# Layer 0's attention: the softmax row sums of two stretches formed in one visit of TensorE

## The chip, the cores and the metric

The kernel runs on one core of one Trainium2 chip, in float32 throughout. The metric is the device time of one execution in microseconds (us). Five engines matter: TensorE (PE, with its weight loads as PEld), VectorE (DVE), ScalarE (ACT), GpSimd (POOL) and the DMA queue that SyncE feeds (SP).

## The reference

Two attention blocks are applied one after the other to 8 images of 512 channels and 1024 positions. The change lies in the first, "layer 0", which has 8 heads of 64 channels:

```python
h = group_norm(x, gn_weight, gn_bias)
qkv = jnp.einsum('oc,bct->bot', w_qkv, h.reshape(B, C, T)) + b_qkv[None, :, None]
...
weight = jnp.einsum('bct,bcs->bts', q * scale, k * scale)
weight = jax.nn.softmax(weight.astype(jnp.float32), axis=-1).astype(weight.dtype)
a = jnp.einsum('bts,bcs->bct', weight, v)
...
out = jnp.einsum('oc,bct->bot', w_proj, a) + b_proj[None, :, None]
return x + out.reshape(B, C, H, W)
```

Layer 1 is of the same kind with one head of 512 channels. The change touches its code only in the form of one call.

## The kernel before

Each image goes through layer 0's attention, the projection, layer 1's products for the image before, and the keys, queries and values for the next one. The four channel tiles of an image hold two heads each. `attention0` (L604) works through 8 stretches per image: a pair of heads hp (0 to 3) by a half of the 1024 positions tb (0 or 1). For hp 0, 1 and 2 the order is tb 0, tb 1; for hp 3 it is tb 1, tb 0. I write a stretch as (hp, tb).

A stretch has two parts on TensorE. First, for each of 8 blocks of 128 keys, it forms the scores `sc` of both heads, each matmul using 64 rows and 128 columns of the array; ScalarE turns them into `e` by Exp (L621), and VectorE adds up the eight `e` tiles into `total` (L623 for the first two, L625 for the rest). Then `av` (128 rows by 64 columns of the array) multiplies `e` by the values and accumulates over the 8 blocks; ScalarE copies it into the channel tile `a` (L639), still without its division by the row sums.

The division goes through `reciprocals` (L575). Four matmuls with `ones` (128 rows by 32 columns) sum `total` over its partitions into one PSUM tile, `sums`, and leave each 128 positions on another group of 32 partitions. VectorE takes the reciprocal (L586), and keeps the smallest (L587, `low_recs`); POOL adds all up (L588, `all_recs`). Both serve a test at the kernel's end. The reciprocals go to DRAM (`rows`, L590) and come back as a broadcast over partitions, `r`, by two DMAs (L600). POOL multiplies `a` by `r` (L644); for the very last stretch of an image, (3, 0), VectorE does so later, and the DMAs go through ScalarE's queue.

Each fp32 matmul stands in the profile as two records: a stretch has 32 records of `sc`, 32 of `av` and 8 of `sums`. Matmuls on different parts of the array run side by side: `sc` and `av` in pairs, `sums` in fours.

The order on TensorE is that of the program, since `matmul` (L67) pins it. Behind the scores and behind `av` of each stretch there is a place for further steps, `extra`: among them, differences of the next operands on VectorE (L1068, `t_h`, `h` and `t_a`), two at a time. On each engine and on the SP queue the instructions stand in program order; a wait on one holds up all behind it.

Tiles come from pools. `total`, `e`, `a` and the operands share one pool of 32 buffers (`big`); `av` and `sums` share two PSUM buffers (`acc`); `rc` and `r` have two buffers each, and `rows` has three.

Of the kernel before, what the change touches and what calls it, by code (L numbers as in the profile page):

```python
# [9 lines left out]
F32 = mybir.dt.float32  # L10
I32 = mybir.dt.int32
AF = mybir.ActivationFunctionType
ALU = mybir.AluOpType
AX = mybir.AxisListType

P = 128
# [13 lines left out]
def two_attention_blocks_kernel(  # L30
# [8 lines left out]
    nc = tc.nc  # L39
    B, C, T = x.shape  # L40
    KC = C // P
    HT = T // 2
# [12 lines left out]
    ones = const.tile([P, P], F32, name="ones")  # L55
# [4 lines left out]
    low_recs = const.tile([P, 2, P], F32, name="low_recs")  # L60
    nc.vector.memset(low_recs, 1.0)
    all_recs = const.tile([P, 2, P], F32, name="all_recs")
# [3 lines left out]
    def matmul(*args, **kw):  # L66
        tc.keep_in_program_order(nc.tensor.matmul(*args, **kw))  # L67
# [108 lines left out]
    def main_path(ctx):  # L176
# [3 lines left out]
        rpool = ctx.enter_context(tc.tile_pool(name="rpool", bufs=2))  # L180
        rowpool = ctx.enter_context(tc.tile_pool(name="rows", bufs=3, space=bass.MemoryType.DRAM))
# [3 lines left out]
        def big_tile(name, shape=(P, T)):  # L185
            return big.tile(list(shape), F32, tag="big", name=name)

        def pair_tile(name):
            return big_tile(name, (P, 2, HT))

        def acc_tile(name):
            return ps_acc.tile([P, HT], F32, tag="acc", name=name)
# [143 lines left out]
        def weight(n):  # L336
            return weight_factors(weight_part(n))
# [53 lines left out]
        def channel_tiles(name):  # L391
            return [big_tile(f"{name}_{c}") for c in range(KC)]
# [23 lines left out]
        def query_factors(f, uid):  # L416

            t = big_tile(f"inner_{uid}", (P, 4, 2 * P))
            s1, s2, s3, s4 = (t[:, i, :] for i in range(4))
            a11, a21, a12, a22 = (f[k][:, ts(i, 2 * P)] for k in range(2) for i in range(2))  # L420
            for dst, x, y, op in (
                (s1, a21, a22, ALU.add), (s2, s1, a11, ALU.subtract), (s3, a11, a21, ALU.subtract),
                (s4, a12, s2, ALU.subtract),
            ):

                tc.keep_in_program_order(nc.gpsimd.tensor_tensor(dst, x, y, op))  # L426
            return {1: a11, 2: a12, 3: s4, 4: a22, 5: s1, 6: s2, 7: s3}
# [144 lines left out]
            return out  # L572


        def reciprocals(total, uid, across, queue=nc.sync):  # L575

            sums = acc_tile(f"sums_{uid}")[:, : 2 * P].rearrange("p (a b) -> p a b", a=2)
            for i in range(4):
                matmul(sums[ts(i, 32), :, :], ones[:, :32], total[:, :, ts(i, P)], start=True, stop=True)
            rc = rpool.tile([P, 2, P], F32, tag="rc", name=f"rc_{uid}")
            nc.vector.reciprocal(rc, sums)  # L586
            nc.vector.tensor_tensor(low_recs, low_recs, rc, ALU.min)  # L587
            nc.gpsimd.tensor_tensor(all_recs, all_recs, rc, ALU.add)  # L588
            rows = rowpool.tile([2, 4, P], F32, tag="rows", name=f"rows_{uid}")
            queue.dma_start(rows.rearrange("j i n -> i j n"), rc[0:P:32, :, :])  # L590
            if across:
                r = pair_tile(f"r_{uid}")
                for j in range(2):
                    row = rows[j : j + 1].rearrange("j i n -> j (i n)")
                    queue.dma_start(r[:, j, :], row.to_broadcast([P, HT]))
            else:
                r = rpool.tile([P, HT], F32, tag="r", name=f"r_{uid}")
                for j in range(2):
                    row = rows[j : j + 1].rearrange("j i n -> j (i n)")
                    queue.dma_start(r[ts(j, 64), :], row.to_broadcast([64, HT]))  # L600
            return r


        def attention0(b, q, k, v, a, extra):  # L604
            n = 0

            for hp in range(KC):
                for tb in (0, 1) if hp < KC - 1 else (1, 0):
                    uid = f"0_{b}_{hp}_{tb}"
                    total = pair_tile(f"sum_{uid}")  # L610
                    es = []
                    for s in range(NS):
                        sc = ps_pools[n % 3].tile([P, 2, HT], F32, tag="sc", name=f"sc_{uid}_{s}")
                        n += 1
                        for j in range(2):
                            matmul(
                                sc[:, j, :], k[hp][ts(j, 64), ts(s, P)], q[hp][ts(j, 64), ts(tb, HT)],
                                start=True, stop=True,
                            )
                        e = pair_tile(f"e_{uid}_{s}")  # L620
                        nc.scalar.activation(e, sc, AF.Exp, scale=(C // 8) ** -0.5)  # L621
                        if s == 1:
                            nc.vector.tensor_add(total, es[0], e)  # L623
                        elif s > 1:
                            nc.vector.tensor_add(total, total, e)  # L625
                        es.append(e)
                    for f in extra.pop(0) if extra else ():
                        f()
                    av = acc_tile(f"av_{uid}")
                    for s in range(NS):  # L630
                        for j in range(2):
                            matmul(
                                av[ts(j, 64), :], v[s // 2][:, s % 2, hp * P + j * 64 : hp * P + (j + 1) * 64],
                                es[s][:, j, :], start=(s == 0), stop=(s == NS - 1),
                            )
                    for f in extra.pop(0) if extra else ():
                        f()
                    dst = a[hp][:, ts(tb, HT)]
                    nc.scalar.copy(dst, av)  # L639

                    last = (hp, tb) == (KC - 1, 0)
                    r = reciprocals(total, uid, False, nc.scalar if last else nc.sync)
                    if not last:
                        nc.gpsimd.tensor_tensor(dst, dst, r, ALU.mult)  # L644
                    else:
                        scaled = lambda dst=dst, r=r: tc.keep_in_program_order(nc.vector.tensor_mul(dst, dst, r))

            assert not extra
            return scaled
# [277 lines left out]
        def load_again(b, c, what):  # L927
            t = big_tile(f"{what}_{b}_{c}")
            nc.sync.dma_start(t, spills[b][c])
            return t  # L930

        def all_background():
            run_background(len(background))
# [93 lines left out]
        def layer1_rest(b, hf, inner, gf, gsteps, stats, hooks, ahead):  # L1027
            if inner:
                first = query_factors(gf[1], f"1_1_{b}")
                total, ef = scores1_twice(b, inner, gf, gsteps, first, f"1_{b}", stats)  # L1030
            else:
                total, ef = scores1(b, gf, hf, f"1_{b}")
            state = {}

            def sums():
                state["r"] = reciprocals(total, f"1_{b}", True)

            z = by_token(
                weight("z"), hf, f"z1_{b}", hooks=[*hooks, [sums]], back=3,
                after=[load_weight, lambda: background.extend(zsteps)],  # L1040
            )
            all_background()
            xt = [load_again(b, c, "x") for c in range(KC)]
            stiles = [big_tile(f"sz{i}_{b}", (P, 2, 2, C // 2)) for i in (1, 2, 4)]
            halves = lambda t: (t[:, :, : C // 2], t[:, :, C // 2 :])
            zf, zsteps = left_sums(
                [halves(t) for t in z[:2]], [halves(t) for t in z[2:]],
                [lambda j, t=t: t[:, j, :, :] for t in stiles], nc.vector.tensor_add, nc.vector.tensor_sub,
            )
            values1(b, zf, ef, state["r"], xt, f"1_{b}", ahead)  # L1050

        for b in range(B):
# [13 lines left out]
            a = channel_tiles(f"a0_{b}")  # L1066
# [4 lines left out]
            if b > 0:  # L1071
                hf, t = image_factors(h, f"h1_{b - 1}", here)
                for i, fs in enumerate((t[:1], t[1:2], (t[2], t[4]), (t[6], t[3]), (t[5], t[7]), steps[:2], steps[2:4])):
                    extra[2 * i + 3] += fs
            elif B > 1:
                hf, t = image_factors(h, "h0_1", here)
# [3 lines left out]
            scaled = attention0(b, q, k, v, a, extra)  # L1080
# [5 lines left out]
            if b > 0:  # L1086
# [6 lines left out]
                _, _, mean, affine = norm_hooks(norm1, f"1_{b}")  # L1093
# [6 lines left out]
                if b + 1 < B:  # L1100
                    hf, steps = image_factors(h, f"h0_{b + 1}")
                    background.extend(steps)
                    v, f, norm0 = values(b + 1, hf)
                    q, k = keys_and_queries(b + 1, f, norm0, ())
            elif B > 1:
                v, f, norm0 = values(1, hf, [[], [], [], [], [*steps[:7], scaled, steps[7]]])
# [169 lines left out]
    with ExitStack() as main_ctx:  # L1276
        main_path(main_ctx)
# [45 lines left out]
```

## Time and profile before

| | |
|---|---|
| median of 3 runs | 2852.84 us (2851.77 to 2853.81) |
| profiled execution, its own time | 2852.44 us |
| its span, first to last instruction | 2850.6 us |
| granted TensorE clock, mean | 0.999 |
| Exp, L621 | 512 times, 1053 ns each |
| adds into `total`, L625 | 384 times, 1357 ns each |
| reciprocal, L586 | 72 times, 1756 ns each |
| `all_recs`, L588 | 72 times, 882 ns each |
| multiply by `r` on POOL, L644 | 56 times, 1943 ns each |

In the timelines that follow, a row is a run of like instructions: its start in us from the span's beginning, the time from its start to the end of its last instruction, engine, line, operation, what it writes and reads, and how many there were; in brackets, how long the engine was idle before it and what ended that. Matmuls are pipelined, so the row of one group reaches into the next; the starts tell more than the ends.

### The profile page before, as it was taken

What the parts mean: (1) busy time and instruction counts of PE and PEld (TensorE: products, weight loads), DVE (VectorE), ACT (ScalarE), POOL (GpSimd) and SP (SyncE); (2) the same over time, 40 slices, a digit from 0 to 9 for tenths busy, and PEclk for the clock granted to TensorE, in tenths of its full rate; (3) what the DMA queues carried; (4) which work ended last, traced back from release to release, by engine and by line L of the source; (5) the groups of instructions that cost most, each with busy time, mean ns of one, the idle gap of its engine ahead of it and who ended that gap; (6) DMA issues with size and microseconds to landing.
All of it is one profiled execution on the core that took longest, in us unless ns stands there. A gap on an engine that the chain in (4) does not pass through costs nothing.

```text
span 2850.6 us, 32020 instructions
## 1 busy us (share of the span) xinstructions
PE 2834.5 (99%) x11720; PEld 1665.7 (58%) x11720; DVE 2062.8 (72%) x2718; ACT 919.9 (32%) x1166; POOL 1106.2 (39%) x1110
## 2 busy tenths in 40 slices
PE   9999999999999999999999999999999999999999
PEld 5435635866367653677537674376833858348544
DVE  5587787766877678776787757877588775887654
ACT  1252452214522145221552215421163312533110
POOL 2113225732167322673127711377114761147100
PEclk9999999999999999999999999999999999999999
DMA  8722403133032231322213231122411224022201
GB/s 276 246 97 90 179 20 134 37 144 126 20 144 76 100 123 42 118 94 97 112 46 111 93 138 72 49 107 101 154 52 45 107 108 153 16 74 79 96 0 68
DMA packets 91594, 281.02 MB, mean 99 GB/s; under 512 B 10595, under 2 KB 36387, under 8 KB 82470
## 3 DMA queue, kind: packets, MB, share of 16 engines
q1 hardware_dynamic: 89638, 276.61, 26.5%
q10 hardware_dynamic: 1792, 2.29, 0.2%
q8 instruction: 95, 1.56, 0.2%
q14 instruction: 69, 0.57, 0.1%
HBM read 225.93 MB, written 52.93 MB: 98 GB/s over the span
## 4 chain that ended last, share of the span: by engine, by line
PE 98%; issue 1%; DVE 1%; POOL 0%; ACT 0%; DVEq 0%; POOLq 0%
PE sc L67 16%; PE av L67 16%; PE psb_av L67 6%; PE psb L67 5%; PE psa_av L67 4%; PE psc_av L67 4%; PE psc L67 3%; PE psa L67 3%; PE psb_z L67 3%; PE psb_p L67 3%; PE psb_v L67 3%; PE psb_g L67 3%; PE psb_k L67 3%; PE psb_q L67 2%; PE psa_p L67 2%; PE psa_z L67 2%
## 5 line engine op out<-in xcount | busy, mean ns | idle before, releaser
L625 DVE TENSOR_TENSOR sum<-sum,e 128x1024 f32<-128x1024 f32 x384 | 521.0, 1357 | 40.7 <-DVE sum L623 0.5
L621 ACT ACTIVATE e<-sc 128x1024 f32<-128x1024 f32 x512 | 476.8, 1053 | 73.4 <-PE sc L67 72.6
L67 PE MATMUL sc<-q,k 64*128 64x512 f32 x2048 | 458.7, 596 | 0.5
L67 PE MATMUL av<-e,v 128*64 128x512 f32 x2048 | 453.6, 595 | 0.0
L67 PEld LDWEIGHTS sc<-q,k 64*128 64x128 f32 x2048 | 193.2, 186 | 239.2 <-ACT e L621 104.0
L67 PEld LDWEIGHTS av<-e,v 128*64 128x64 f32 x2048 | 141.4, 137 | 304.3 <-issue 304.3
L588 POOL TENSOR_TENSOR all_recs<-all_recs,rc 128x256 f32<-128x256 f32 x72 | 63.5, 882 | 579.6 <-DVE rc L586 572.0
L644 POOL TENSOR_TENSOR a<-a,r 128x512 f32<-128x512 f32 x56 | 108.8, 1943 | 260.8 <-DMA r<-rows 246.5
L586 DVE RECIPROCAL rc<-sums 128x256 f32<-128x256 f32 x72 | 126.4, 1756 | 47.8 <-PE sums L67 26.6
L532 POOL TENSOR_TENSOR k<-k,k 128x256 f32<-128x256 f32 x28 | 20.0, 726 | 314.5 <-DVE u_k L527 314.5
L639 ACT COPY a<-av 128x512 f32<-128x512 f32 x64 | 37.4, 585 | 322.7 <-PE av L67 322.7
L623 DVE TENSOR_TENSOR sum<-e,e 128x1024 f32<-128x1024 f32 x64 | 78.4, 1226 | 59.3 <-ACT e L621 59.3
L67 PE MATMUL psa_av<-e,z 128*128 128x512 f32 x256 | 113.3, 595 | 0.0
L140 ACT ACTIVATE h<-h,b,s 128x1024 f32<-128x1024 f32 x62 | 78.5, 1270 | 87.2 <-DMA h<-in_x 70.6
L67 PE MATMUL psb<-inner,inner_h 128*128 128x256 f32 x392 | 101.6, 382 | 0.8
L411 POOL TENSOR_TENSOR inner_h<-h,inner_h 128x256 f32<-128x256 f32 x112 | 101.1, 905 | 2.2
L67 PEld LDWEIGHTS psb<-inner,inner_h 128*128 128x128 f32 x392 | 73.3, 190 | 14.9 <-POOL inner L426 3.4
L67 PEld LDWEIGHTS psa_av<-e,z 128*128 128x128 f32 x256 | 48.0, 190 | 57.3 <-issue 56.6
L411 POOL TENSOR_TENSOR inner_h<-h 128x256 f32<-128x256 f32 x56 | 55.4, 990 | 66.8 <-ACT h L140 66.8
L411 POOL TENSOR_TENSOR inner_h<-t_h 128x256 f32<-128x256 f32 x84 | 73.6, 879 | 10.8 <-PE psc_av L67 9.5
L67 PE MATMUL psb_g<-inner_h,w_m 128*128 128x256 f32 x294 | 75.1, 383 | 0.3
L67 PE MATMUL psb_q<-inner_h,w_q 128*128 128x256 f32 x294 | 75.4, 385 | 0.0
(382 smaller groups left out, 5435.2 us busy)
## 6 DMA issues: line engine op xcount, KB each, us to landing
x<-in_x SPq DMA_DIRECT2D x36, 512.0 KB
h<-in_x SPq DMA_DIRECT2D x32, 512.0 KB
spill<-x SPq DMA_DIRECT2D x32, 512.0 KB
h<-spill SPq DMA_DIRECT2D x32, 512.0 KB
x<-spill SPq DMA_DIRECT2D x32, 512.0 KB
out<-x SPq DMA_DIRECT2D x64, 256.0 KB
w_p<-sums_p SPq DMA_DIRECT2D x8, 1792.0 KB
r<-rows SPq DMA_DIRECT2D x112, 128.0 KB
```

The lines of the kernel that those rows point to most:

```text
L67: tc.keep_in_program_order(nc.tensor.matmul(*args, **kw))
L140: tc.keep_in_program_order(nc.scalar.activation(dst, src, AF.Identity, bias=b, scale=s))
L411: pin(nc.gpsimd.tensor_tensor(dst, x, y, ALU.subtract))
L532: nc.gpsimd.tensor_tensor(d, x, y, ALU.add)
L586: nc.vector.reciprocal(rc, sums)
L588: nc.gpsimd.tensor_tensor(all_recs, all_recs, rc, ALU.add)
L621: nc.scalar.activation(e, sc, AF.Exp, scale=(C // 8) ** -0.5)
L623: nc.vector.tensor_add(total, es[0], e)
L625: nc.vector.tensor_add(total, total, e)
L639: nc.scalar.copy(dst, av)
L644: nc.gpsimd.tensor_tensor(dst, dst, r, ALU.mult)
```

## The change

`reciprocals` takes a list of totals. For `n` of them it forms `n` groups of sums, side by side in one PSUM tile, and returns `n` tiles `r`. `attention0` keeps (`total`, `dst`) of the stretches (0, 0), (1, 0) and (2, 0), which are listed in `PAIRS_BEGUN`, and calls `reciprocals` for two totals after (0, 1), (1, 1) and (2, 1). Both stretches of hp 3 call it with one total, as before. Layer 1 calls it with one total.

```diff
-        def reciprocals(total, uid, across, queue=nc.sync):
+        def reciprocals(totals, uid, across, queue=nc.sync):
...
-            sums = acc_tile(f"sums_{uid}")[:, : 2 * P].rearrange("p (a b) -> p a b", a=2)
-            for i in range(4):
-                matmul(sums[ts(i, 32), :, :], ones[:, :32], total[:, :, ts(i, P)], start=True, stop=True)
-            rc = rpool.tile([P, 2, P], F32, tag="rc", name=f"rc_{uid}")
-            nc.vector.reciprocal(rc, sums)
-            nc.vector.tensor_tensor(low_recs, low_recs, rc, ALU.min)
-            nc.gpsimd.tensor_tensor(all_recs, all_recs, rc, ALU.add)
-            rows = rowpool.tile([2, 4, P], F32, tag="rows", name=f"rows_{uid}")
-            queue.dma_start(rows.rearrange("j i n -> i j n"), rc[0:P:32, :, :])
...
+            n = len(totals)
+            sums = acc_tile(f"sums_{uid}")[:, : n * 2 * P].rearrange("p (t a b) -> p t a b", t=n, a=2)
+            for t, total in enumerate(totals):
+                for i in range(4):
+                    matmul(sums[ts(i, 32), t, :, :], ones[:, :32], total[:, :, ts(i, P)], start=True, stop=True)
+            rs = []
+            for t in range(n):
+                rc = rpool.tile([P, 2, P], F32, tag="rc", name=f"rc_{uid}_{t}")
+                nc.vector.reciprocal(rc, sums[:, t, :, :])
+                nc.vector.tensor_tensor(low_recs, low_recs, rc, ALU.min)
+                nc.gpsimd.tensor_tensor(all_recs, all_recs, rc, ALU.add)
+                rows = rowpool.tile([2, 4, P], F32, tag="rows", name=f"rows_{uid}_{t}")
+                queue.dma_start(rows.rearrange("j i n -> i j n"), rc[0:P:32, :, :])
...
+                else:
+                    r = rpool.tile([P, HT], F32, tag="r", name=f"r_{uid}_{t}")
+                    for j in range(2):
+                        row = rows[j : j + 1].rearrange("j i n -> j (i n)")
+                        queue.dma_start(r[ts(j, 64), :], row.to_broadcast([64, HT]))
+                rs.append(r)
+            return rs
...
+        PAIRS_BEGUN = [(hp, 0) for hp in range(KC - 1)]
...
-                    last = (hp, tb) == (KC - 1, 0)
-                    r = reciprocals(total, uid, False, nc.scalar if last else nc.sync)
-                    if not last:
-                        nc.gpsimd.tensor_tensor(dst, dst, r, ALU.mult)
-                    else:
-                        scaled = lambda dst=dst, r=r: tc.keep_in_program_order(nc.vector.tensor_mul(dst, dst, r))
+                    unscaled.append((total, dst))
+
+                    if (hp, tb) not in PAIRS_BEGUN:
+
+                        last = (hp, tb) == (KC - 1, 0)
+                        rs = reciprocals([t for t, _ in unscaled], uid, False, nc.scalar if last else nc.sync)
+                        for (_, dst), r in zip(unscaled, rs):
+                            if not last:
+                                nc.gpsimd.tensor_tensor(dst, dst, r, ALU.mult)
+                            else:
+                                scaled = lambda dst=dst, r=r: tc.keep_in_program_order(nc.vector.tensor_mul(dst, dst, r))
+                        unscaled = []
...
-                state["r"] = reciprocals(total, f"1_{b}", True)
+                (state["r"],) = reciprocals([total], f"1_{b}", True)
```

The order of the instructions in the changed program follows from this and from a scheduler that fills engines in between. On VectorE, the two reciprocals of a pair stand first, then the two `low_recs`; on POOL, two `all_recs`, then two multiplies; on the SP queue, two `rows`, then the four `r`.

More of the change, by code (lines that the diff above doesn't have):

```diff
@@ L572, in conv2 @@
             return out
-        def reciprocals(total, uid, across, queue=nc.sync):
-            sums = acc_tile(f"sums_{uid}")[:, : 2 * P].rearrange("p (a b) -> p a b", a=2)
-            for i in range(4):
-                matmul(sums[ts(i, 32), :, :], ones[:, :32], total[:, :, ts(i, P)], start=True, stop=True)
-            rc = rpool.tile([P, 2, P], F32, tag="rc", name=f"rc_{uid}")
-            nc.vector.reciprocal(rc, sums)
-            nc.vector.tensor_tensor(low_recs, low_recs, rc, ALU.min)
-            nc.gpsimd.tensor_tensor(all_recs, all_recs, rc, ALU.add)
-            rows = rowpool.tile([2, 4, P], F32, tag="rows", name=f"rows_{uid}")
[L590 to L595, printed above, removed]
-            else:
[L597 to L601, printed above, removed]
@@ new lines, in reciprocals @@
+        def reciprocals(totals, uid, across, queue=nc.sync):
[12 more added lines that the diff above has]
+                queue.dma_start(rows.rearrange("j i n -> i j n"), rc[0:P:32, :, :])
+                if across:
+                    r = pair_tile(f"r_{uid}_{t}")
+                    for j in range(2):
+                        row = rows[j : j + 1].rearrange("j i n -> j (i n)")
+                        queue.dma_start(r[:, j, :], row.to_broadcast([P, HT]))
+                else:
+                    r = rpool.tile([P, HT], F32, tag="r", name=f"r_{uid}_{t}")
+                    for j in range(2):
+                        row = rows[j : j + 1].rearrange("j i n -> j (i n)")
+                        queue.dma_start(r[ts(j, 64), :], row.to_broadcast([64, HT]))
+                rs.append(r)
+            return rs
@@ L639, in attention0 @@
                     nc.scalar.copy(dst, av)
-                    last = (hp, tb) == (KC - 1, 0)
-                    r = reciprocals(total, uid, False, nc.scalar if last else nc.sync)
-                    if not last:
-                        nc.gpsimd.tensor_tensor(dst, dst, r, ALU.mult)
-                    else:
-                        scaled = lambda dst=dst, r=r: tc.keep_in_program_order(nc.vector.tensor_mul(dst, dst, r))
+                    unscaled.append((total, dst))
[7 more added lines that the diff above has]
+                                scaled = lambda dst=dst, r=r: tc.keep_in_program_order(nc.vector.tensor_mul(dst, dst, r))
+                        unscaled = []
             assert not extra
```

## The prediction, made before the changed kernel ran

> **What bounds the kernel now.** I read the busy times first, then the chain that ended last, then the timeline of one stretch, engine by engine.
>
> ```profile
> PE 2834.5 (99%) x11720; PEld 1665.7 (58%) x11720; DVE 2062.8 (72%) x2718; ACT 919.9 (32%) x1166; POOL 1106.2 (39%) x1110
> ...
> PE 98%; issue 1%; DVE 1%; POOL 0%; ACT 0%; DVEq 0%; POOLq 0%
> ```
>
> TensorE is the bound: every microsecond it gains or waits moves the end. The timeline of PE over stretch (3,1) of image 3, i.e. hp 3, tb 1, the one that follows the third pair:
>
> ```profile
> 1113.68 0.60 PE L67 MATMUL av<-e,v 128*64 128x512 f32 x2
> 1114.21 0.64 PE L67 MATMUL sums<-sum,ones 128*32 128x256 f32 x8
> 1114.78 7.14 PE L67 MATMUL sc<-q,k 64*128 64x512 f32 x32
> 1121.85 7.09 PE L67 MATMUL av<-e,v 128*64 128x512 f32 x32
> 1128.87 0.64 PE L67 MATMUL sums<-sum,ones 128*32 128x256 f32 x8
> ```
>
> A stretch takes 14.66 us (1114.21 to 1128.87) and PE never rests in it. The same stretch on DVE, POOL and the SP queue:
>
> ```profile
> 1114.97 1.76 DVE L586 RECIPROCAL rc<-sums 128x256 f32<-128x256 f32 x1 [0.36 <-issue]
> 1116.77 0.43 DVE L587 TENSOR_TENSOR low_recs<-low_recs,rc 128x256 f32<-128x256 f32 x1
> 1117.93 1.23 DVE L623 TENSOR_TENSOR sum<-e,e 128x1024 f32<-128x1024 f32 x1 [0.74 <-ACT e L621]
> 1119.26 8.75 DVE L625 TENSOR_TENSOR sum<-sum,e 128x1024 f32<-128x1024 f32 x6
> 1127.93 1.29 DVE L1068 TENSOR_TENSOR t_a<-a 128x512 f32<-128x512 f32 x2
> ```
> ```profile
> 1116.88 0.90 POOL L588 TENSOR_TENSOR all_recs<-all_recs,rc 128x256 f32<-128x256 f32 x1 [7.20 <-DVE rc L586]
> 1122.16 2.11 POOL L644 TENSOR_TENSOR a<-a,r 128x512 f32<-128x512 f32 x1 [4.38 <-DMA r<-rows]
> ```
> ```profile
> 1116.76 0.57 SPq L590 DMA_DIRECT2D rows<-rc  x1
> 1118.47 1.10 SPq L600 DMA_DIRECT2D r<-rows  x2
> ```
>
> DVE is the engine to watch. It starts the stretch with the reciprocal of the stretch before, idles 0.74 us for the second exp, adds up the eight e tiles, and is done at 1119.26+8.75 = 1128.01. TensorE wants that total at 1128.87: 0.86 us to spare. So DVE's whole reserve in a stretch is 0.74+0.86 = 1.60 us. Six adds took 8.75 us here; in a stretch of image 0 into which no POOL multiply falls, six took 7.87:
>
> ```profile
> 139.84 7.87 DVE L625 TENSOR_TENSOR sum<-sum,e 128x1024 f32<-128x1024 f32 x6
> ```
>
> One multiply by r costs DVE 0.88 us. Of the group's durations (minimum, median, maximum), the maximum is what the unluckiest single add took:
>
> ```profile
> L625 DVE TENSOR_TENSOR sum<-sum,e x384: 1224/1225/2347, 125.2 to 2533.3; 128x1024 f32<-128x1024 f32 x192
> ```
>
> **What the Trainium skill says.** "TensorEngine Tiling (Array Packing)", Key Properties: a change of tiling mode drains TensorE. The trace agrees: the last av pair is 0.53 us ahead of the sums (1113.68 to 1114.21), where av pairs within a stretch follow each other at 0.429. "TensorE: Matmul & The Clock Gate", LDWEIGHTS: a load takes the number of columns by 1/1.2 ns, 107, 53 and 27 ns for 128, 64 and 32. The trace agrees here too: after a switch the second group of matmuls is late by 104 ns (sc), 51 (av) and 26 (sums), as if that one load were uncovered. "SBUF — State Buffer", Who interferes with whom: a VectorE instruction with two SBUF inputs and a GpSimd instruction that reads SBUF lock each other out. That is the 0.88 us above; a reciprocal, with one input from PSUM, is not touched (1.76 us in all 72 cases).
>
> **Part 1: the sums of tb 0 leave their place.** This happens in hp 0, 1 and 2 of 8 images: 24 boundaries. By single records of PE's timeline, from the last av pair to the second sc pair it now takes 0.523 (drain) + 0.569 (sums) + 0.533 (first sc pair) = 1.625 us. Left is a direct switch from av to sc, which no place in this kernel shows. Every switch seen costs about 0.093 to drain, and every entry into 128-column weights 0.104, so I take 0.523+0.533 = 1.056 us. Gain 0.569 a boundary. Bounds: 0.55, if the exit takes the 0.115 seen after sums; 0.77, if av to sc needs no drain and no uncovered load.
>
> **Part 2: they stand before the sums of tb 1.** Eight more PE records in two passes, no new switch. Two passes of 256 columns are 2 x 0.214 = 0.43 us (half of 0.429 each). Bounds 0.43 and 0.48 (26 ns more each). No wait: that total has been ready for a stretch. Net gain 0.569-0.43 = 0.14 us a pair, 24 x 0.14 = 3.3 us; with the bounds 1.7 to 8.
>
> **Part 3: everything behind the sums doubles in one place.** Count, place, order, cost:
> - DVE: the order becomes reciprocal, reciprocal, low_recs, low_recs, then the adds of the next stretch. A stretch after a pair carries 1.76+0.43 us more, the second of the pair that much less.
> - POOL: two all_recs, then two multiplies, in the stretch after the pair.
> - SP: rows, rows, r, r, r, r. The first r is queued behind the second rows, which waits for the second reciprocal. Nothing on PE waits for r here; the multiply only lands later.
> - Buffers: a total of tb 0 is held a stretch longer, but every e tile still takes over one whose last reader is at least half a stretch back, so I book nothing for ACT.
>
> In the stretches (1,0) and (2,0), the first of a pair, DVE may be late: no sums stand at their end any more, the next stretch has no reciprocal ahead of it, and DVE's spare time there takes the delay up. Stretch (3,1) is the exception: it follows the third pair, and its sums are wanted at its own end. Call the start of the third pair's sums S:
> - The sums end 0.43 later, so the first reciprocal starts at S + 0.76 + 0.43 = 1.19 (now 1114.97-1114.21 = 0.76).
> - Two reciprocals with 0.03 between them: to 4.74. First low_recs to 5.20, the second from 5.30. The second all_recs starts about 0.14 after the second reciprocal and runs 0.90 to 5.78, across the second low_recs, which then ends near 6.07 (5.73 if not locked out). The first add starts at 6.11. The exps, which now start it at 3.72, give no excuse: they come at 4.15.
> - Seven adds with no multiply: 1.22 + 0.10 + 7.87 = 9.19. Two multiplies at 0.88: 1.76. The first can start once r lands, by the SP lines about 3.4 us after its second issue, at S+9.2; the second follows it to about S+13.4. Both fall among the adds.
> - Last add at 6.11+9.19+1.76 = S+17.06; about 0.1 to signal (estimate from the 0.14 between reciprocal and all_recs).
> - TensorE gets there at 14.66+0.43 = S+15.08. It waits 17.16-15.08 = 2.1 us.
>
> Queued behind the waiting sums on PE are the whole of (3,0) and all that follows; nothing may overtake. So 8 x 2.1 = 16.6 us are added, one per image. Bounds of the wait: 1.2 if one multiply misses the adds, 2.55 if both hit as badly as the 2.35 us add. After the wait, DVE does its two t_a steps while PE starts again, and its reciprocal comes some 0.4 later than now, inside the 0.74 of idle time; (3,0) keeps its reserve.
>
> **Sum.** Against the profiled execution: 2852.44 - 3.3 + 16.6 = 2865.7 us. Its own time is 0.40 below the median of the runs, 2852.84, so I forecast 2866.1.
>
> **Rivals.**
> - Smaller collision: one multiply misses the adds or the second low_recs isn't locked out. Wait 1.2 to 1.75; with 1.2, 2852.8-3.3+9.6 = 2859.1. For it: where r lands is inferred. Against: all 7 adds lie between S+6 and S+17, with r due at about 9 and 10.
> - No wait, so not slower: DVE catches up and only parts 1 and 2 remain, 2849.5; with a free switch from av to sc 2845. It decides once the last add ends before S+15.0, 2.1 us earlier than I get. That takes both multiplies (1.76) and the low_recs lock (0.34) out of DVE's way together. For it: DVE is only 72% busy over the span. Against: in this stretch it is 88% busy (12.91 of 14.66) before anything is added.
> - The clock: 2 us without a matmul, and TensorE is throttled. "TensorE: Matmul & The Clock Gate", Part 1, speaks of an idle window of about 3.4 us; no run here shows one. At half rate for 3.4 us, 1.7 us more per image: 2880.
> - The change doesn't do what it says: the two groups of sums don't run on as one, and the second costs a full 0.569. Then the gain is nothing and the time 2869.4, inside my range.
>
> **How the numbers follow.** Forecast 0.74 (the last rival in it), smaller collision 0.13, no wait 0.09, clock 0.04. Low end 2857, which takes in the smaller collision with a gain above my value; high end 2871, the 2.55 us wait (20.4) with a gain of 1.7 (2852.8+20.4-1.7). What is left out is about 0.15. A measurement of this kernel can tell about 0.2%, 5.7 us. Slower by more: the forecast, half of the smaller collision, the clock: 0.85. Faster by more: the free switch alone, 0.03. Within: 0.12.
>
> **What would show it.** Right: no sums after tb 0 of hp 0 to 2, and 16 sums records of about 1.07 us after tb 1; in (3,1), last add near S+17 and the sums' weight load waiting about 2 us for "DVE sum", 8 times; PE gapless elsewhere. Wrong: sums of (3,1) at S+15.1, multiplies outside the adds, PE waiting in (1,0) or (2,0), or a granted clock below 0.99.

## The result and the profile after

| | before | after |
|---|---|---|
| median, 8 runs each | 2852.61 us (2851.77 to 2853.81) | 2861.81 us (2860.63 to 2863.70) |
| ratio after to before | | 1.0031, 95% interval 1.0023 to 1.0040 |
| profiled execution, its own time | 2852.44 us | 2861.88 us |
| its span | 2850.6 us | 2860.1 us |
| granted TensorE clock, mean | 0.999 | 0.999 |

The change makes the kernel 9.2 us slower. First the busy times, the chain that ended last and the longest wait of PE, in the profile after:

```profile
PE 2832.0 (99%) x11720; PEld 1668.9 (58%) x11720; DVE 2062.7 (72%) x2718; ACT 919.9 (32%) x1166; POOL 1096.6 (38%) x1110
...
PE 93%; DVE 3%; ACT 2%; issue 1%; POOL 0%; DMA 0%; DVEq 0%; SPq 0%; ACTq 0%; POOLq 0%
...
PE sums L67 <- DVE sum L633: 12.0, 8, 1.5
```

PE's busy time hardly changes (2.5 us less), but the chain is no longer all PE: it runs through DVE and ACT for 5% of the span, in the stretches that end in a wait. ACT's share doesn't mean that the exps came late: in the stretch below the last of them ends at 1126.40, and the add that needs it starts at 1132.15. The last line is the whole story in short: 12.0 us in all, 8 times, 1.5 us at the longest, always `sums` for DVE's last add into `total` (L633 is L625 of before; line numbers differ between the kernels).

Stretch (3,1) of image 3 again, PE first:

```profile
1115.83 1.03 PE L67 MATMUL av<-e,v 128*64 128x512 f32 x4
1116.79 1.07 PE L67 MATMUL sums<-sum,ones 128*32 128x256 f32 x16
1117.79 7.14 PE L67 MATMUL sc<-q,k 64*128 64x512 f32 x32
1124.85 7.09 PE L67 MATMUL av<-e,v 128*64 128x512 f32 x32
1133.43 0.64 PE L67 MATMUL sums<-sum,ones 128*32 128x256 f32 x8 [1.49 <-DVE sum L633]
```

Sixteen records of sums stand where eight stood; they take 1.00 us to the next sc (1116.79 to 1117.79), 0.43 more than 0.57. The stretch's own sums, at the end, come after a pause of 1.49 us, which before was none. The same stretch on DVE and POOL:

```profile
1117.98 3.37 DVE L590 RECIPROCAL rc<-sums 128x256 f32<-128x256 f32 x2 [1.73 <-issue]
1121.26 1.23 DVE L591 TENSOR_TENSOR low_recs<-low_recs,rc 128x256 f32<-128x256 f32 x2
1122.42 1.21 DVE L631 TENSOR_TENSOR sum<-e,e 128x1024 f32<-128x1024 f32 x1
1123.74 9.64 DVE L633 TENSOR_TENSOR sum<-sum,e 128x1024 f32<-128x1024 f32 x6
1133.29 1.29 DVE L1081 TENSOR_TENSOR t_a<-a 128x512 f32<-128x512 f32 x2
```
```profile
1119.88 0.72 POOL L592 TENSOR_TENSOR all_recs<-all_recs,rc 128x256 f32<-128x256 f32 x1 [19.42 <-DVE rc L590]
1121.49 0.72 POOL L592 TENSOR_TENSOR all_recs<-all_recs,rc 128x256 f32<-128x256 f32 x1 [0.89 <-DVE rc L590]
1125.86 3.77 POOL L656 TENSOR_TENSOR a<-a,r 128x512 f32<-128x512 f32 x2 [3.65 <-DMA r<-rows]
```

DVE doesn't idle before its first add any more. The six adds take 9.64 us, where one multiply on POOL made them 8.75: both multiplies lie between 1125.86 and 1129.63, among the adds. The last add ends at 1133.38 and the sums start at 1133.43.

From the single records, each of the eight waits is 1.56 to 1.57 us (the distance from the last av pair, less the 0.522 that it takes without a wait), 12.5 in all. Each of the 24 boundaries without sums takes 0.523+0.533 us, the direct switch as it was assumed. So 12.5 - 24 x (0.569-0.431) = 9.2 us, against 9.2 between the medians and 9.4 between the profiled executions.

### The profile page after: what moved, and what is told of

It is laid out like the page before. It is cut to its first block, busy times and chain, and to the rows that moved or that the text cites. A ratio compares the mean times of both kernels' runs of the same rounds, so it can differ in the third digit from the quotient of the medians.

```text
span 2860.1 us, 32039 instructions
## 1 busy us (share of the span) xinstructions
PE 2832.0 (99%) x11720; PEld 1668.9 (58%) x11720; DVE 2062.7 (72%) x2718; ACT 919.9 (32%) x1166; POOL 1096.6 (38%) x1110
## 3 DMA queue, kind: packets, MB, share of 16 engines
q8 instruction: 95, 1.56, 0.2%
## 4 chain that ended last, share of the span: by engine, by line
PE 93%; DVE 3%; ACT 2%; issue 1%; POOL 0%; DMA 0%; DVEq 0%; SPq 0%; ACTq 0%; POOLq 0%
PE sc L67 14%; PE av L67 14%; PE psb_av L67 6%; PE psb L67 5%; PE psa_av L67 4%; PE psc_av L67 4%; PE psb_z L67 3%; PE psc L67 3%; PE psa L67 3%; PE psb_p L67 3%; PE psb_g L67 3%; PE psb_k L67 3%; PE psb_v L67 3%; PE psb_q L67 2%; PE psa_p L67 2%; PE psa_z L67 2%
## 5 line engine op out<-in xcount | busy, mean ns | idle before, releaser
L633 DVE TENSOR_TENSOR sum<-sum,e 128x1024 f32<-128x1024 f32 x384 | 519.1, 1352 | 41.1 <-DVE sum L633 0.5
L592 POOL TENSOR_TENSOR all_recs<-all_recs,rc 128x256 f32<-128x256 f32 x72 | 54.8, 761 | 727.4 <-DVE rc L590 727.4
```

## The experiments

The theory after the result, A: sharing a visit saves TensorE 0.14 us, anywhere; the single sums that come first after a pair wait 1.56 us, since VectorE finishes their total too late, and POOL's two multiplies are what tips it. Rivals: sharing itself costs something at every pair (B), only (3,1) is tight (C), POOL has little to do with it (D). Two more, E and F, come up in later expectations.

### Only the third pair

```diff
-        PAIRS_BEGUN = [(hp, 0) for hp in range(KC - 1)]
+        PAIRS_BEGUN = [(KC - 2, 0)]
```

> Only the third pair of stretches, (2,0) and (2,1), shares its sums. Theory A (each shared visit saves TensorE 0.137 us; the single sums that follow a pair wait 1.56 us for VectorE's last add): 8 x 1.56 - 8 x 0.137 = 11.4 us over the kernel before, about 2864.0, slower than the changed kernel; eight waits of the sums for DVE in the trace. Rival B (every shared pair costs about the same, 9.2 us over 24 pairs = 0.39 each): 8 x 0.39 = 3.1 us over, about 2855.7.

2864.54 us against 2852.83 before (ratio 1.0042, 1.0027 to 1.0057). As A has it, B is out: two thirds of the shared visits are gone, and the kernel is not faster for it. The trace has eight waits of 1.56 to 1.57 us.

### The first two pairs

```diff
-        PAIRS_BEGUN = [(hp, 0) for hp in range(KC - 1)]
+        PAIRS_BEGUN = [(0, 0), (1, 0)]
```

> The first two pairs share their sums, hp 2 and hp 3 sum each stretch by itself. Theory A: it is the first single stretch after a pair that waits, so the wait moves to (2,0): 8 x 1.56 - 16 x 0.137 = 10.3 us over the kernel before, about 2862.9. Rival C (only (3,1) has too little room, for its place at the end of the attention): no wait, 16 x 0.137 = 2.2 us under, about 2850.4.

2863.77 us (ratio 1.0038, 1.0025 to 1.0052), as A has it; C is out. Seven of the eight waits are 1.56 to 1.57 us, one is 1.91. PE's timeline in image 3 shows where the wait went:

```profile
1087.51 1.07 PE L67 MATMUL sums<-sum,ones 128*32 128x256 f32 x16
1088.51 7.14 PE L67 MATMUL sc<-q,k 64*128 64x512 f32 x32
1095.58 7.09 PE L67 MATMUL av<-e,v 128*64 128x512 f32 x32
1104.16 0.64 PE L67 MATMUL sums<-sum,ones 128*32 128x256 f32 x8 [1.50 <-DVE sum L633]
1104.73 7.14 PE L67 MATMUL sc<-q,k 64*128 64x512 f32 x32
1111.80 7.09 PE L67 MATMUL av<-e,v 128*64 128x512 f32 x32
1118.82 0.64 PE L67 MATMUL sums<-sum,ones 128*32 128x256 f32 x8
```

The single sums right behind a pair, now those of (2,0), wait; the next single ones don't. It is not a place in the image but the order "pair, then single".

### The third pair's multiplies after the adds

```diff
+                    if waiting:
+                        tc.keep_in_program_order(nc.gpsimd.tensor_copy(seen, total[:, 0, 0:1]))
+                        for d, r in waiting:
+                            tc.keep_in_program_order(nc.gpsimd.tensor_tensor(d, d, r, ALU.mult))
+                        waiting = []
                     for f in extra.pop(0) if extra else ():
...
-                            if not last:
+                            if (hp, tb) == (KC - 2, 1):
+                                waiting.append((dst, r))
+                            elif not last:
```

> Three pairs as in the changed kernel; the third pair's two multiplies by r on POOL wait, behind a one-column copy out of the finished total, until the adds of (3,1) are done. Theory A (two multiplies lock VectorE's adds out for 1.76 us, more than the 1.56 us that the sums wait): last add near 14.8 us after the pair's sums instead of 16.6, no wait of the sums, 24 x 0.137 = 3.3 us under the kernel before, about 2849.3; the multiplies then lie between the stretches and may cost (3,0) up to 0.5 us of its room. Rival D (the doubled reciprocals and minima alone use the room up, POOL hardly matters): the wait stays, about 2861.8.

2849.82 us, ratio 0.9989 (0.9982 to 0.9996) to the kernel before: the only version here that beats both the kernel before and the changed one. Nothing on VectorE, TensorE or the queues was taken out; POOL's multiplies stand elsewhere, behind a copy of one column that has to wait for the total. D is out. VectorE and TensorE in the same stretch of image 3:

```profile
1117.52 1.21 DVE L633 TENSOR_TENSOR sum<-e,e 128x1024 f32<-128x1024 f32 x1
1118.83 7.88 DVE L635 TENSOR_TENSOR sum<-sum,e 128x1024 f32<-128x1024 f32 x6
1126.63 1.29 DVE L1090 TENSOR_TENSOR t_a<-a 128x512 f32<-128x512 f32 x2
```
```profile
1111.88 1.07 PE L67 MATMUL sums<-sum,ones 128*32 128x256 f32 x16
...
1126.96 0.64 PE L67 MATMUL sums<-sum,ones 128*32 128x256 f32 x8
```

The six adds take 7.88 us instead of 9.64, and the sums come 15.08 us after the pair's, with no wait in brackets. The only wait left in all eight images is one of 0.20 us, in image 0's last stretch, where POOL's next work also falls among the adds. What is left is the forecast's parts 1 and 2, 3.3 us, less that wait: 3.1 us by the spans (2847.5 against 2850.6), 3.0 by the medians.

### One multiply left out

```diff
+                            if (hp, tb) == (KC - 2, 1) and dst is unscaled[1][1]:
+                                continue
                             if not last:
```

> Three pairs as in the changed kernel, but the second multiply by r of the third pair is left out, so the second half of channel tile 2 stays undivided. Theory A: one multiply less among the adds takes 0.88 us off the wait of 1.56, leaving 0.68: 8 x 0.68 - 3.3 = 2.1 us over the kernel before, about 2854.7. Rival D (POOL hardly matters): about 2861.8.

2854.66 us (ratio 1.0006, 0.9997 to 1.0014): 1.8 us over the kernel before, which is not clear of the noise. The waits show the change plainly: 0.68 us, eight times. One multiply is worth 1.56-0.68 = 0.88 us of the wait, as its six adds show: 8.76 us where the changed kernel has 9.64.

### The minima left out

```diff
-                nc.vector.tensor_tensor(low_recs, low_recs, rc, ALU.min)
+                if not uid.endswith("_2_1"):
+                    nc.vector.tensor_tensor(low_recs, low_recs, rc, ALU.min)
```

> Three pairs as in the changed kernel, but the two low_recs minima of the third pair are left out, so the test at the kernel's end misses them. Theory A with the spacings of the changed kernel's trace: the first add of (3,1) starts at 4.48 us after the pair's sums instead of 5.64, everything behind it 1.16 earlier, so the sums wait 1.56 - 1.16 = 0.41: 8 x 0.41 - 3.3 = 0, about 2852.7, level with the kernel before. With the prediction's own figures (each step after the end of the one before, minima from 4.77 to 6.07) the same edit takes 1.33 us off: 8 x 0.77 - 3.3 = 2.9 over, about 2855.6.

2855.36 us (ratio 1.0009, 1.0000 to 1.0018), 2.8 over the kernel before; the waits are 0.69 us. The figures that theory A took from the trace missed, and those of the prediction fit by accident. VectorE and POOL show why:

```profile
1119.24 1.16 DVE L632 TENSOR_TENSOR sum<-e,e 128x1024 f32<-128x1024 f32 x1
1120.50 9.96 DVE L634 TENSOR_TENSOR sum<-sum,e 128x1024 f32<-128x1024 f32 x6
```
```profile
1119.46 1.51 POOL L593 TENSOR_TENSOR all_recs<-all_recs,rc 128x256 f32<-128x256 f32 x1 [0.89 <-DVE rc L590]
```

The first add came when it was due, 4.48 us after the pair's sums (1119.24-1114.76). But POOL's second `all_recs`, begun during that add, now takes 1.51 us instead of 0.72 and makes the next add late in turn: the first of the six takes 1.56 us instead of 1.23, and all six 9.96, 0.32 more than in the changed kernel. A part of what the lock cost had only moved to another instruction.

### Reciprocal and minimum in turn

```diff
-                nc.vector.reciprocal(rc, sums[:, t, :, :])
-                nc.vector.tensor_tensor(low_recs, low_recs, rc, ALU.min)
+                tc.keep_in_program_order(nc.vector.reciprocal(rc, sums[:, t, :, :]))
+                tc.keep_in_program_order(nc.vector.tensor_tensor(low_recs, low_recs, rc, ALU.min))
```

> The changed kernel with reciprocal, minimum, reciprocal, minimum in this order on VectorE instead of both reciprocals first. Theory A: the second minimum now comes before POOL's second all_recs and isn't locked out (0.43 us instead of 0.84), which outweighs that a minimum which waits for its reciprocal can't overlap it: first add at about 5.47 us after the pair's sums instead of 5.64, 0.17 less wait, 8 x 0.17 = 1.3 us under the changed kernel, about 2860.5. Rival E (the lock doesn't touch so short an instruction, the 0.84 has another cause): the two lost overlaps of 0.08 to 0.1 us each make the first add later, about 5.8, and the time 1 us over the changed kernel, about 2863.

2874.37 us (ratio 1.0081, 1.0064 to 1.0097): both theories missed, by 11 us or more. The trace, of stretch (3,1) of image 3, shows three things. First, the lock again:

```profile
1123.48 0.43 DVE L591 TENSOR_TENSOR low_recs<-low_recs,rc 128x256 f32<-128x256 f32 x1
1123.82 1.75 DVE L631 TENSOR_TENSOR sum<-e,e 128x1024 f32<-128x1024 f32 x1
```

The second minimum is indeed not locked out (0.43 us), but the add behind it is (1.75 instead of 1.22). The wait of the sums grows to 1.92 us here and to 1.92 to 2.05 in the eight images, 15.6 in all. Second, the edit also pinned the order in layer 1, and TensorE now waits for VectorE there, as this line of PE's waits tells (us in all, times, longest):

```profile
PE psb_av L67 <- DVE u_av L238: 2.2, 5, 0.6
```

Third, TensorE's clock. This table by stages (busy times of PE, PEld, DVE, ACT and POOL, then the granted clock, DMA share and GB/s) begins just after a wait in image 3:

```profile
1135.40:1136.40 1.00, 1.00 (x10) 0.42 (x12) 1.00 (x2) 0.00 (x0) 0.00 (x0) 1.00 0.00 0
1136.40:1139.60 3.20, 3.20 (x10) 1.39 (x8) 2.21 (x3) 1.31 (x2) 0.90 (x1) 0.50 0.00 1
```

The clock is at half for 3.4 us, and sc pairs follow each other at 0.85 us instead of 0.43. It happens after two of the eight waits, and each time the way from the sums to `av` takes 9.33 us instead of 7.64, so a drop of the clock costs 1.7 us.

The profiled execution took 2870.94 us, and its span is 18.4 us over that before; 15.6 of waits, 2.2 in layer 1 and 3.4 for the clock, less 3.3, make 17.9. Its granted clock was 0.998 in the mean; the other three runs, 3.2 to 7.0 us slower, had 0.997. More drops of the clock would fit that, but no trace shows them.

### In turn, in layer 0 alone

```diff
-                nc.vector.reciprocal(rc, sums[:, t, :, :])
-                nc.vector.tensor_tensor(low_recs, low_recs, rc, ALU.min)
+                pin = (lambda i: i) if across else tc.keep_in_program_order
+                pin(nc.vector.reciprocal(rc, sums[:, t, :, :]))
+                pin(nc.vector.tensor_tensor(low_recs, low_recs, rc, ALU.min))
```

> As in_turn, but layer 1's reciprocals keep the scheduler's order; only layer 0 has reciprocal, minimum, reciprocal, minimum. Theory A, mended after in_turn (POOL's second all_recs locks out whichever two-input VectorE instruction comes next, a 1.2 us add now instead of a 0.4 us minimum): the sums of (3,1) wait 1.92 us as in in_turn, 8 x 1.92 - 3.3 = 12.1 us over the kernel before, about 2864.7, and 1.6 us more for each time that TensorE's clock drops after a wait (in_turn's trace has two such drops); no wait of psb_av for VectorE in layer 1. Rival F (the order within layer 0 costs all of in_turn's time): about 2871 to 2874.

2867.92 us (ratio 1.0053, 1.0037 to 1.0070; 2866.01 to 2870.70). The waits are 1.91 to 1.96 us, and PE no longer waits for VectorE in layer 1. The profiled execution, 2870.70 us, has four drops of the clock, each of 1.7 us again and not the 1.6 that was expected. Its span is 18.3 us over that before; 15.4 of waits, less 3.3, and 4 x 1.7 for the clock make 18.9, 0.6 too many. The median, 15.7 over, fits two drops. Only a profiled execution shows their number, but the granted clocks of the other three runs go the same way: 0.998 for 2869.38 us, 0.999 for 2866.47 and 2866.01. F is out: the median lies below its forecast, and the 2.2 us of waiting in layer 1 are gone. The slowest run comes near it, through the clock.

### POOL's all_recs left out

```diff
-                nc.gpsimd.tensor_tensor(all_recs, all_recs, rc, ALU.add)
+                if not uid.endswith("_2_1"):
+                    nc.gpsimd.tensor_tensor(all_recs, all_recs, rc, ALU.add)
```

> The changed kernel with POOL's two all_recs additions of the third pair left out, so the test at the kernel's end misses them. Theory A (the second all_recs locks the second minimum out): that minimum takes 0.43 us instead of 0.84, the first add starts at 5.22 us after the pair's sums instead of 5.64, the sums wait 1.56 - 0.41 = 1.15: 8 x 1.15 - 3.3 = 5.9 us over the kernel before, about 2858.5. Rival E (the 0.84 has another cause): as the changed kernel, about 2861.8.

2859.26 us against 2852.20 (ratio 1.0025, 1.0014 to 1.0035), 7.1 over where 5.9 was expected; the span is 7.5 over. The waits are 1.14 to 1.21 us, the expected 1.15, and the two minima take 0.82 us instead of 1.23. So the second `all_recs` had locked the second minimum out. E is out. The waits sum up to 9.3, less 3.3 is 6.0. Most of the rest lies in layer 1: PE's list of waits has one for VectorE there that the lists of before and after don't have, `psb_av` for `w_av`, twice, 1.6 us in all. Why leaving out two additions of POOL brings it about isn't shown.

## Why the prediction was right, and where it was off

- **Part 1 and 2, right in size.** The direct switch from av to sc, which no row of before showed, costs what the two halves of other switches cost: 0.523 and 0.533 us, 24 times. The added sums take 0.43. The gain shows in the kernel with late multiplies: 3.0 to 3.1 us, with 0.2 of waiting against it. One reading beside it was loose: the prediction says that the trace agrees with weight loads of 107, 53 and 27 ns. What agrees is how late the second group of matmuls is (104, 51, 26); the load records themselves last 183 to 187, 132 to 137 and 106 to 109 ns.
- **Part 3, right in place.** The wait is in (3,1), once per image, for the last add; none in (1,0) or (2,0), where no sums stand at the end; TensorE doesn't wait in (3,0) either.
- **The term that was mis-sized: the wait, 2.1 us forecast, 1.56 measured**, over the eight images 16.6 against 12.5, which is nearly all of the 4.3 us between forecast and median. The adds and multiplies were right: 10.95 us from first to last forecast, 10.96 measured. The first add was not: forecast at S+6.11, measured at S+5.64. There the prediction laid VectorE's instructions end to end, and even with 0.03 to 0.1 between them. But the first minimum, which needs nothing from the second reciprocal, started at S+4.48, while that reciprocal ended at S+4.56; the second reciprocal and the first add started 0.08 ahead of an end too. The profile before had shown such overlaps, here an instruction of 0.68 us with the next one 0.60 behind its start:

```profile
1113.33 0.68 DVE L1068 TENSOR_TENSOR h<-h,h 128x512 f32<-128x512 f32 x1
1113.93 0.69 DVE L1068 TENSOR_TENSOR t_h<-h,t_h 128x512 f32<-128x512 f32 x1
```

The Trainium skill, "VectorE: DVE Perf Modes", The DRAIN you can't avoid, says too that an instruction which isn't held starts before the one ahead has drained. The signal from VectorE to TensorE took 0.055 where 0.1 was taken.

- **The lock on the second minimum, right, and shown** by leaving out `all_recs`. The measured wait lies in the band of the rival with the smaller collision, but not for its reason: both multiplies hit, and the minimum was locked out.
- **No wait, and so no slowdown:** the prediction asked for both multiplies and the lock on the minimum to be out of VectorE's way together, 2.1 us. Since the wait was only 1.56, the multiplies alone (1.76) are enough: the kernel with late multiplies takes 2849.82 us, where the prediction had 2849.5.
- **The clock** stayed at full in the changed kernel's profiled execution. That was luck: the prediction gave a drop a chance of 0.04 with waits of 2.1 us, and waits of 1.91 to 2.05 brought it about 6 times in 16. The changed kernel was spared by waits shorter than forecast: none of 23 waits of 1.56 to 1.57 brought a drop.
- **The rival in which the second group of sums doesn't run on behind the first** is out: 16 records take 1.00 us to the next sc, 0.43 more than 8.

## What to carry to other kernels

Where the bound engine saves a little by batching the small work of others, look for the first place at which the batch's follow-up must be done before that engine's next need, and add up there everything that stands in line, busy shares over the span apart: here 3 x 0.14 us of gain stood against 1.56 us of waiting at one place in each image. A multiply of POOL that fell among VectorE's two-input adds cost VectorE 0.88 us here, so such work belongs in VectorE's sum; here it could be placed behind the need by a cheap read of what had to be finished first. And where an instruction that was locked out was taken away or moved, a part of the delay fell on the next one: 0.32 us without the minima, 0.53 with reciprocal and minimum in turn.

## What the runs showed of the hardware that was not expected

TensorE's clock fell to half for 3.41 us after 6 of 16 waits of 1.91 to 2.05 us (two kernels), and after none of 23 waits of 1.56 to 1.57 (three kernels); a single wait of 1.91 in the kernel with two pairs did not bring it about either. Each drop cost 1.7 us, nearly the wait once more. The prediction had leaned on the Trainium skill, "TensorE: Matmul & The Clock Gate", Part 1, with its idle window of about 3.4 us; the pause that is enough now and then is shorter here, and the measurement decides.

The record of the granted clock shows a part of what decides in the single case. In each of the two kernels the starts of the drops lie whole multiples of 3.4133 us apart (1402.88 us is 411 of them; 563.20, 1399.46 and 351.57 us are 165, 410 and 103), so they divide time into steps of that length. Each of the six waits with a drop lies for at least 1.91 us in a single step and begins no later than 0.9 us into it. Nine of the other eleven are cut by a border between steps, with at most 1.82 us in either (one of them in the kernel with two pairs, where the clock's rise at the start marks the steps). The last two lie whole in one step but begin 1.2 and 1.5 us into it; why they brought no drop these runs don't show.
